# Row statistics moved from VectorE to ScalarE, in whole rows, and one combination from GpSimd to VectorE

## The chip, the cores and the metric

The kernel runs on one core of a Trainium2 chip. A core has TensorE (matrix products into the accumulation memory, PSUM), VectorE, ScalarE and GpSimd for elementwise work, and SyncE, which issues almost all transfers between the device memory and the on-chip memory, SBUF. Each engine works through its own queue in the order in which the program wrote it; engines meet through semaphores. In the profile they are called PE (and PEld for its weight loads), DVE, ACT, POOL and SP. The metric is the device time of one execution in microseconds; the time before is 2860.64 us, the median of 3 runs (2856.56 to 2867.07).

## What is computed

x is 128 batches of 128 tokens with 768 features; adj is 128 matrices of 128 x 128 edge weights, most of them zero. Per batch the kernel computes a normalised and clipped x, one attention layer with 12 heads of 64 features masked by the edges, and adds the result to x:

```
h      = maximum(layernorm(x), 0)                  # mean and variance over the 768 features of a token
q, k, v = h @ Wq + bq, h @ Wk + bk, h @ Wv + bv    # 768 x 768 each, split into 12 heads
scores = q @ k.T / sqrt(64) + beta * adj           # per head, 128 x 128
scores = where(adj > 0, scores, -9e15)
out    = x + softmax(scores) @ v
```

Everything is float32. The layer norm needs two numbers for each token, its mean and its variance; these are the row statistics of the title. The row sums of the title are the denominators of the softmax: each v has a 65th column of ones, so the product of exponentials and v carries the sum of the exponentials in that column.

## The kernel before

**Groups, slices and products.** The 128 batches are taken in 32 groups of four. For each group the projections are computed in three slices of columns: qk0 (q and k of the first six heads), v, and qk1 (q and k of the last six). Each slice is a fast product of 2 x 3 blocks of activations with 3 x 3 blocks of weights, with 15 block products (`PRODUCTS`) in place of 18; each block product in turn uses seven half-size products, called zones, in place of eight. So a slice is 15 positions, taken in the order `ZORDER` (qk0 and v) or `QORDER` (qk1), and a group is 45 positions. Order of slices in the steady loop: qk0, v, qk1, then qk0 of the next group.

The operands of a product are a sum of activation blocks (prepared on VectorE and GpSimd by `sum_acts` and `inner`) and a sum of weight blocks. The weight sums are made once; 11 of the 45 stay in SBUF and 34 are read again for each group from device memory through a ring of five buffers (`load_T`, 448 KB each). The load of the next one is issued by SyncE when a product has freed its buffer, that is, some seven positions ahead of its use.

**Chains and homes.** Each product belongs to one of four chains a, b, c, d (third column of `PRODUCTS`) and is accumulated on top of the products of its chain in one pair of PSUM banks; there are four pairs. The next product of a chain overwrites what the readers of the one before still need, so TensorE waits until they have read. The readers are in `product_z`. Each output block (r, j) has a home in SBUF, seven zones wide. The first product that touches a home is copied there, mainly by ScalarE (lines 560, 563 and 565; two zones of v by VectorE, line 559); each further one is added by VectorE (line 569). When a home is complete, `decode` combines its seven zones into four, on GpSimd (lines 585 to 588 for q and k, 596 to 600 for v), one or four positions later. In ZORDER position 6 copies into a home of v, position 9 is on chain a as position 6 is, and position 13 is on chain d as position 10 is. In QORDER position 0 opens two homes at once, with two runs of lines 563 and 565, and position 3 is the next product of its chain, d.

**Attention.** `scores` makes the products of q and k for two heads of the four batches (line 622), `mask` adds the edge bias on VectorE (line 630), ScalarE takes the exponential (line 632). `attend` multiplies with v between the zones of a product (line 675); ScalarE copies the result with its row sums out of PSUM (line 684, which frees the bank pair); two positions later `weigh` clips and inverts the sums on VectorE (lines 645 and 646), ScalarE scales by them (line 658), VectorE adds x (line 698). The scores and the attention of the second half of a group's heads are interleaved with qk0 of the next group: scores at positions 3, 5 and 6.

**Layer norm.** Activations are read in a transposed block form, 32 tokens at a time, by `load_x`; `norm` applies scale, shift and clipping on ScalarE (line 446), and `to_hT` transposes on VectorE (line 457). The scale and shift come from statistics of the plain rows: for group G + 2, during slice v of group G (for group 2, during qk0 of group 1), `load_half` reads each batch in two halves of 384 features into three buffers in turn, `half_stats` takes VectorE's statistics of a half (line 415) and joins two halves (line 417), and `row_moments` turns the eight results into scale and shift (lines 423 to 430), which are brought into the block form through device memory.

**Order.** The order of the work is written out by hand. `run` goes through the positions; `then(at, f, ...)` puts f behind the matmuls of position `at`, and `then((at, "post"), ...)` behind its evacuation and behind the exponentials and scalings that trail it. What is put there takes its place in the queue of whichever engine it runs on: a load in SyncE's, ahead of the weight load of the next position.

Of the kernel before, what the change touches and what calls it, by code (L numbers as in the profile page):

```python
# [125 lines left out]
def direct(ctx, tc, x, adj, wq, bq, wk, bk, wv, bv, beta, out, bad):  # L126
# [39 lines left out]
    def flat(lo, hi):  # L166
        return sbig[:, lo:hi]
# [36 lines left out]
    ones = const.tile([P, P], F32, name="ones")  # L204
    nc.gpsimd.memset(ones, 1.0)
    beta_s = const.tile([P, 1], F32, name="beta_s")

# [190 lines left out]

    def load_half(G, n):

        g, h = n // 2, n % 2
        if n % 3 == 2:
            t = work.tile([P, VH], F32, tag="adj", name=f"half_{G}_{g}_{h}", bufs=1)
        else:
            t = half_homes[n % 3]
        rows[G, g, h] = t
        nc.sync.dma_start(t, x[G * GRP + g, :, h * VH:(h + 1) * VH])

    def half_stats(G, n):

        g, h = n // 2, n % 2
        if n == 0:
            rows[G] = stat.tile([P, GRP, 2, nc.vector.BN_STATS_DIM], F32, tag="strow", name=f"strow_{G}", bufs=1)
            rows[G, "mv"] = stat.tile([P, GRP, nc.vector.BN_AGGR_DIM], F32, tag="mvrow", name=f"mvrow_{G}", bufs=1)
        nc.vector.bn_stats(rows[G][:, g, h, :], rows.pop((G, g, h)))  # L415
        if h:
            nc.vector.bn_aggr(rows[G, "mv"][:, g, :], rows[G][:, g])

    def row_moments(G, first=5, then=8):

        mv = rows[G, "mv"]
# [107 lines left out]
    def product_z(G, sl, n):  # L529
# [21 lines left out]
        for (r, j), sign in uses:  # L551
# [85 lines left out]

    def weigh(G, oc, pa, o):

        n = pa.shape[1]  # L640
# [3 lines left out]
        t = sums[G][:, oc]  # L644
        nc.vector.tensor_scalar(t[:, 0, 0:n], pa[:, :, :, HD], TINY, None, op0=ALU.max)
        nc.vector.reciprocal(t[:, 1, 0:n], t[:, 0, 0:n])  # L646
# [18 lines left out]
    def attend_steps(G, oc, behind):  # L665
# [16 lines left out]

        def leave_pair():
            nc.scalar.copy(o.rearrange("p r b e -> p r (b e)"), pair[:, :, 0:4 * VE])  # L684
            give(pair)
            later(weighed_later, 2)

        def weighed_later():
            divide = weigh(G, oc, o, o)
# [350 lines left out]
    for G in range(1, NG):  # L1040
# [6 lines left out]
        if G == 1:  # L1047
            sums_at(1, ((0, "S6"), (1, "S7"), (2, "S0"), (5, "S5"), (7, "S14"), (9, "S11")))
            then((0, "post"), load_x, 2, 0)
            for n, at in enumerate((1, 1, 1, 6, 8, 9, 11, 11)):  # L1050
                then((at, "post"), load_half, 2, n)
            for n, at in enumerate((6, 8, 9, 10, 11, 12, 13, 14)):
                then(at, half_stats, 2, n)
            then(14, row_moments, 2, 3, 5)
# [14 lines left out]
        if more:  # L1069
            then((11, "post"), add_raw, G + 1)  # L1070
            if G == 1:
                for g in range(2):
                    then((6 + g, "post"), norm, 2, g)
                turn_act(2, ((9, "A01"), (10, "A00"), (11, "A02")), 1)
                then((11, "post"), load_x, 2, 1)
                then((14, "post"), norm, 2, 2)
# [17 lines left out]
        if G == 1:  # L1094
            then((0, "post"), norm, 2, 3)
# [160 lines left out]
```

## Time and profile before

| | |
|---|---|
| median of 3 runs | 2860.64 us (2856.56 to 2867.07) |
| profiled execution | 2872.12 us, span 2870.3 us, mean granted TensorE clock 0.984 |
| TensorE busy | 2727.4 us, 95% of the span |
| VectorE busy | 2319.8 us, 81% |
| GpSimd busy | 2202.8 us, 77% |
| ScalarE busy | 1496.6 us, 52% |
| transfers | 721.72 MB, mean 251 GB/s |
| chain that ended last, by engine | GpSimd 42%, TensorE 27%, VectorE 12%, DMA 11% |

The prediction quotes lines of the profile. A group line gives the line of the kernel, the engine, the operation, output and input tiles with their shapes and the count; then busy time in us and the mean of one in ns; then the idle time of the engine just ahead of these instructions, and what ended it. A line of the waits names who waited for whom, with the total in us, the times and the longest. A line of the timeline gives start and length in us, and in square brackets an idle time ahead of it with its releaser. A line of transfers gives the tile, the count, the size and the median time from issue to landing. A busy share is a mean over the span; a wait counts where it stops the engine that is the bound. The lines of before: L415 and L417 are the statistics of halves, L645 the clipping of row sums, L585 to L588 the combination of a q/k home.

### The profile page before, as it was taken

To read this page: it belongs to the slowest core of one execution; us is meant where nothing else is said; L and a number is where in the kernel's file an instruction comes from. 1 tells how busy PE (TensorE), PEld (TensorE's weight loads), DVE (VectorE), ACT (ScalarE), POOL (GpSimd) and SP (SyncE) were. 2 spreads that over 40 slices of the span, in tenths; PEclk is the share of its full clock that TensorE was granted. 3 is DMA by queue.
4 is the path that set the end of the run, shared out by engine and by line. 5 is a ranking of instruction groups with operands and counts; after the bars stand their busy time and mean duration, and the time that the engine had idled before them with its cause. 6 is when DMAs were issued, how large, how long until landed. Compare 5 with 4: busy or idle time off the path is not lost.

```text
span 2870.3 us, 121387 instructions
## 1 busy us (share of the span) xinstructions
PE 2727.4 (95%) x52029; PEld 2598.4 (91%) x52029; DVE 2319.8 (81%) x3148; ACT 1496.6 (52%) x3823; POOL 2202.8 (77%) x3169
## 2 busy tenths in 40 slices
PE   9989999999999999999999999999999999999998
PEld 7789998999999999989899999899898999998997
DVE  6878888887878788888788888788887887878885
ACT  1455655455555555554555554555545555555654
POOL 4667878777878778787778787778787787877885
PEclk9999999999999999999999999999999999999999
DMA  8779878888888898788888888888887888978875
GB/s 214 252 241 275 263 238 270 247 262 260 232 260 262 250 268 263 239 270 251 250 274 248 253 265 253 259 258 239 263 263 244 267 236 251 273 240 266 247 229 164
DMA packets 547620, 721.72 MB, mean 251 GB/s; under 512 B 107900, under 2 KB 406664, under 8 KB 547080
## 3 DMA queue, kind: packets, MB, share of 16 engines
q1 hardware_dynamic: 545920, 713.13, 82.2%
q8 instruction: 412, 6.75, 0.9%
q10 hardware_dynamic: 1160, 0.79, 0.1%
q14 instruction: 128, 1.05, 0.1%
HBM read 647.73 MB, written 66.05 MB: 249 GB/s over the span
## 4 chain that ended last, share of the span: by engine, by line
POOL 42%; PE 27%; DVE 12%; DMA 11%; issue 4%; ACT 2%; SPq 0%; POOLq 0%; DVEq 0%; ACTq 0%
PE pair L545 22%; DMA sbig<-in_x_dram 9%; POOL home L586 6%; POOL home L588 5%; POOL home L585 4%; POOL v L600 4%; DVE home L569 4%; POOL home L587 4%; POOL home L598 4%; PE pair L675 3%; DVE strow L415 3%; POOL v L599 3%; PE pair L622 2%; POOL A L467 2%; POOL home L597 2%
## 5 line engine op out<-in xcount | busy, mean ns | idle before, releaser
L569 DVE TENSOR_TENSOR home<-home,pair 128x896 f32<-128x896 f32 x810 | 857.9, 1072 | 200.2 <-PE pair L545 177.6
L545 PE MATMUL pair<-sbig,T_qk 128*64 128x128 f32 x13888 | 887.3, 273 | 3.3 <-DMA T_qk<-kept_qk 1.7
L545 PEld LDWEIGHTS pair<-sbig,T_qk 128*64 128x64 f32 x13888 | 754.7, 137 | 17.2 <-issue 10.0
L658 ACT ACTIVATE e<-e,sm 128x64 f32<-128x64 f32 x1512 | 382.2, 339 | 242.1 <-DVE sm L646 242.1
L545 PE MATMUL pair<-A,T_qk 128*64 128x128 f32 x6076 | 425.0, 278 | 0.0
L585 POOL TENSOR_TENSOR home<-home 128x256 f32<-128x256 f32 x325 | 259.1, 797 | 215.8 <-DVE home L569 213.0
L545 PE MATMUL pair<-T_v,sbig 128*64 128x128 f32 x6944 | 413.8, 274 | 3.0 <-DVE sbig L569 3.0
L675 PE MATMUL pair<-v,e 128*64 128x65 f32 x6048 | 404.1, 223 | 2.8 <-DVE e L630 2.8
L545 PEld LDWEIGHTS pair<-T_v,sbig 128*64 128x64 f32 x6944 | 385.0, 137 | 8.6 <-issue 5.3
L563 ACT ACTIVATE home<-pair 128x640 f32<-128x640 f32 x325 | 228.3, 703 | 303.1 <-PE pair L545 299.0
L675 PEld LDWEIGHTS pair<-v,e 128*64 128x64 f32 x6048 | 363.3, 139 | 6.8 <-DVE e L630 3.3
L545 PEld LDWEIGHTS pair<-A,T_qk 128*64 128x64 f32 x6076 | 338.9, 140 | 5.5 <-issue 5.3
L588 POOL TENSOR_TENSOR home<-home 128x256 f32<-128x256 f32 x325 | 291.4, 897 | 25.5
L586 POOL TENSOR_TENSOR home<-home 128x256 f32<-128x256 f32 x325 | 289.7, 891 | 25.5
L632 ACT ACTIVATE e<-e 128x1024 f32<-128x1024 f32 x189 | 200.3, 1060 | 185.0 <-DVE e L630 172.7
L630 DVE SCALAR_TENSOR_TENSOR e<-pair,biasT 128x1024 f32<-128x1024 f32 x189 | 229.8, 1216 | 61.4 <-PE pair L622 61.0
L684 ACT COPY e<-pair 128x520 f32<-128x520 f32 x189 | 111.5, 590 | 316.7 <-PE pair L675 316.7
L446 ACT ACTIVATE x<-x,block 128x192 f32<-128x192 f32 x480 | 231.8, 543 | 10.2 <-DMA x<-in_x_dram 10.2
L622 PE MATMUL pair<-home 64*64 64x128 f32 x5312 | 201.1, 279 | 36.4 <-POOL home L587 23.4
L587 POOL TENSOR_TENSOR home<-home 128x128 f32<-128x128 f32 x325 | 207.8, 639 | 25.5
L467 POOL TENSOR_TENSOR A<-A 128x256 f32<-128x256 f32 x186 | 153.2, 824 | 89.2 <-DVE A L457 89.1
L545 PE MATMUL pair<-T_v,A 128*64 128x128 f32 x2604 | 167.0, 281 | 56.4 <-DVE home L569 47.7
(178 smaller groups left out, 4616.2 us busy)
## 6 DMA issues: line engine op xcount, KB each, us to landing
T_qk<-kept_qk SPq DMA_DIRECT2D x713, 448.0 KB, 4.8
T_v<-kept_v SPq DMA_DIRECT2D x341, 448.0 KB, 5.7
xo<-in_x_dram SPq DMA_DIRECT2D x189, 256.0 KB, 4.3
out_dram<-xo SPq DMA_DIRECT2D x189, 256.0 KB, 5.7
x<-in_x_dram SPq DMA_DIRECT2D x248, 192.0 KB, 5.8
sbig<-in_x_dram SPq DMA_DIRECT2D x186, 192.0 KB, 5.2
half<-in_x_dram SPq DMA_DIRECT2D x60, 192.0 KB, 3.9
kept_qk<-prep_qk SPq DMA_DIRECT2D x23, 448.0 KB, 3.1
```

What stands on the lines that cost most here:

```text
L446: nc.scalar.activation(t, t, AF.Relu, bias=shift[G, n], scale=rstd[G, n])
L545: nc.tensor.matmul(p[q:q + HD, at, :], lhs[:, q:q + HD], rhs, start=(first and at % 4 == 0), stop=True, skip_group_check=True)
L563: nc.scalar.activation(t[:, 0:5], p[:, 0:5], AF.Copy, scale=float(sign))
L569: nc.vector.tensor_tensor(t, t, p[:, 0:7], op)
L585: e.tensor_tensor(t[:, 1:4:2], t[:, 1:4:2], twice(5), ALU.add)
L586: e.tensor_tensor(t[:, 2:5:2], t[:, 2:5:2], twice(1), ALU.add)
L587: e.tensor_tensor(t[:, 4], t[:, 4], t[:, 6], ALU.add)
L588: e.tensor_tensor(t[:, 0:7:6], t[:, 0:7:6], twice(2), ALU.add)
L622: nc.tensor.matmul(ps[k:k + HD, i, g * N:(g + 1) * N], keys[r, k:k + HD], queries[r], start=True, stop=True)
L630: nc.vector.scalar_tensor_tensor(e, ps, SCORE_CAP * ISCALE, bias, op0=ALU.min, op1=ALU.add)
L658: nc.scalar.activation(o[:, r, b, 0:HD], pa[:, r, b, 0:HD], AF.Copy, scale=t[:, 1, r, b:b + 1])
L675: nc.tensor.matmul(pa[q:q + HD, 2 * g + i, :], k[:, q:q + HD], vt[G, "v", r, h // 4][:, 4 * g + h % 4, :], start=True, stop=True, skip_gro ...
```

## The change

Three edits, with the positions of the work around them moved to fit:

- **Row statistics.** A whole row of 768 features is read into one buffer, where the first two half-row buffers stood (the third, in the tile `adj`, is no longer used). ScalarE makes two passes over it, both written back in place: a copy that accumulates the sum, then a square of the row less its mean that accumulates the squared deviations; between them a multiplication of one column makes the negative mean. `row_moments` takes these. A row can be loaded when the second pass over the row before has ended. In the steady loop the first row of a group is loaded at position 12 of qk0, the others at 2, 6 and 11 of v; the statistics stand behind positions 1, 5, 10 and 14 of v. The normalisations of the second pair of batches move from positions 5, 6, 8, 9 of v to 3, 4, 7, 8.
- **Row sums.** ScalarE reads the column of sums from PSUM, adds 1e-30 and writes it, ahead of the copy of line 684; VectorE's clipping (line 645) goes, except in the last group's half-size steps.
- **One combination.** The home completed by product 13 of qk1 (position 12), block (1, 2), is combined by VectorE in place of GpSimd.

```diff
-    half_homes = [flat(spare + i * D // 2, spare + (i + 1) * D // 2) for i in range(2)]
+    row_home = flat(spare, spare + D)
...
+    def load_row(G, g):
+        nc.sync.dma_start(row_home, x[G * GRP + g])
+
+    def row_stats(G, g):
+
+        if g == 0:
+            rows[G] = stat.tile([P, 3, GRP], F32, tag="strow", name=f"strow_{G}", bufs=1)
+        s = rows[G]
+        nc.scalar.activation(row_home, row_home, AF.Copy, accum_out=s[:, 0, g:g + 1])
+        nc.scalar.mul(s[:, 1, g:g + 1], s[:, 0, g:g + 1], -1.0 / D)
+        nc.scalar.activation(row_home, row_home, AF.Square, bias=s[:, 1, g:g + 1], accum_out=s[:, 2, g:g + 1])
...
-        nc.vector.tensor_scalar(ve, mv[:, :, 1], EPS, None, op0=ALU.add)
-        mean = stat.tile([P, GRP], F32, tag="meanrow", name=f"meanrow_{G}", bufs=1)
-        nc.vector.tensor_scalar(mean, mv[:, :, 0], -1.0, None, op0=ALU.mult)
+        nc.vector.tensor_scalar(ve, rows[G][:, 2], 1.0 / D, EPS, op0=ALU.mult, op1=ALU.add)
+        mean = rows[G][:, 1]
...
-                later(lambda r=r, j=j: decode(G, sl, r, j), 1 if order_of(G, sl) is LORDER else LAG.get((sl, n), 1))
+                later(lambda r=r, j=j: decode(G, sl, r, j, nc.vector if (sl, n) == ("qk1", 13) else nc.gpsimd), 1 if order_of(G, sl) is LORDER else LAG.get((sl, n), 1))
...
         def leave_pair():
+            nc.scalar.activation(row_sums(G, oc)[:, 0], pair[:, :, 0:4 * VE].rearrange("p r (b e) -> p r b e", e=VE)[:, :, :, HD],
+                                 AF.Identity, bias=tiny)
             nc.scalar.copy(o.rearrange("p r b e -> p r (b e)"), pair[:, :, 0:4 * VE])
...
+                if G + 2 < NG:
+                    then((12, "post"), load_row, G + 2, 0)
...
-                for n, at in enumerate((5, 6, 8, 9)):
+                for n, at in enumerate((3, 4, 7, 8)):
                     then((at, "post"), norm, G + 1, 2 + n // 2, n % 2 * 2, n % 2 * 2 + 2)
...
-                for n, at in enumerate((0, 0, 0, 4, 4, 5, 7, 9)):
-                    then((at, "post"), load_half, G + 2, n)
-                for n, at in enumerate((4, 4, 5, 7, 9, 9, 11, 12)):
-                    then(at, half_stats, G + 2, n)
+                for g, at in enumerate((0, 4, 8, 11) if G == 1 else (None, 2, 6, 11)):
+                    if at is not None:
+                        then((at, "post"), load_row, G + 2, g)
+                for g, at in enumerate((3, 6, 10, 14) if G == 1 else (1, 5, 10, 14)):
+                    then((at, "post"), row_stats, G + 2, g)
```

Group 1, which prepares group 2 in its own qk0 slice, has other positions for the same work: rows loaded at 1, 5, 9 and 12 of qk0 with the statistics at 4, 8, 11 and 14, `row_moments` moved from position 14 of qk0 to 0 of v, the first two normalisations of group 2 at 7 and 8 of v (before 6 and 7), its transpositions and the load of its second pair one position later each, and the third normalisation moved from v to qk1.

More of the change, by code (lines that the diff above doesn't have):

```diff
@@ L205, in direct @@
     nc.gpsimd.memset(ones, 1.0)
+    tiny = const.tile([P, 1], F32, name="tiny")
+    nc.gpsimd.memset(tiny, TINY)
     beta_s = const.tile([P, 1], F32, name="beta_s")
@@ L636, in direct, with row_sums @@
     sums, weighed = {}, {}
-    def weigh(G, oc, pa, o):
-        n = pa.shape[1]
+    def row_sums(G, oc):
         if G not in sums:
@@ L643, in weigh @@
             weighed[G] = 0
-        t = sums[G][:, oc]
-        nc.vector.tensor_scalar(t[:, 0, 0:n], pa[:, :, :, HD], TINY, None, op0=ALU.max)
+        return sums[G][:, oc]
+    def weigh(G, oc, pa, o, summed=False):
+        n = pa.shape[1]
+        t = row_sums(G, oc)
+        if not summed:
+            nc.vector.tensor_scalar(t[:, 0, 0:n], pa[:, :, :, HD], TINY, None, op0=ALU.max)
         nc.vector.reciprocal(t[:, 1, 0:n], t[:, 0, 0:n])
@@ L1049, in direct @@
             then((0, "post"), load_x, 2, 0)
[L1050 to L1054, printed above, removed]
+            for g, at in enumerate((1, 5, 9, 12)):
+                then((at, "post"), load_row, 2, g)
+            for g, at in enumerate((4, 8, 11, 14)):
+                then((at, "post"), row_stats, 2, g)
         else:
@@ L1071, in direct @@
             if G == 1:
+                then(0, row_moments, 2, 3, 5)
                 for g in range(2):
[L1073 to L1076, printed above, removed]
+                    then((7 + g, "post"), norm, 2, g)
+                turn_act(2, ((10, "A01"), (11, "A00"), (12, "A02")), 1)
+                then((12, "post"), load_x, 2, 1)
             else:
-                for n, at in enumerate((5, 6, 8, 9)):
+                for n, at in enumerate((3, 4, 7, 8)):
                     then((at, "post"), norm, G + 1, 2 + n // 2, n % 2 * 2, n % 2 * 2 + 2)
@@ L1094, in direct @@
         if G == 1:
-            then((0, "post"), norm, 2, 3)
+            for g in range(2, GRP):
+                then((g - 2, "post"), norm, 2, g)
             turn_act(2, ((3, "A10"), (4, "A11"), (5, "A12")), 1)
```

19 lines of the change are left out of this document (1 added, 18 removed).

## The prediction

> **What bounds the kernel now.** I read the page's busy shares first, then TensorE's waits, then one group stage by stage and in order of time. All prices below belong to one steady group of four batches: the one whose v slice begins at 1131 us.
>
> ```profile
> PE 2727.4 (95%) x52029; PEld 2598.4 (91%) x52029; DVE 2319.8 (81%) x3148; ACT 1496.6 (52%) x3823; POOL 2202.8 (77%) x3169
> ```
> ```profile
> PE pair L545 <- DVE home L569: 48.0, 26, 2.0
> PE pair L622 <- POOL home L587: 23.4, 21, 1.2
> PE pair L545 <- DVE e L630: 12.0, 20, 1.5
> PE pair L545 <- DVE sbig L569: 11.8, 6, 3.0
> PE pair L622 <- POOL home L588: 10.3, 27, 0.5
> ```
> TensorE is busy 95% of the span, so no edit to another engine can win more than its waits and what they do to its clock. The five rows of TensorE's waits (us, times, longest) sum to 105.5 us. They come once a group each, at two places: a product of the v slice waits for VectorE, and the scores in the next qk0 slice wait for GpSimd.
>
> In order of time (start us, us, [idle before <- releaser]), first TensorE, then VectorE:
>
> ```profile
> 1148.58 1.70 PE L545 MATMUL pair<-T_v,sbig 128*64 128x128 f32 x28
> ...
> 1156.96 1.75 PE L545 MATMUL pair<-T_v,A 128*64 128x128 f32 x28 [1.97 <-DVE home L569]
> ...
> 1164.65 1.70 PE L545 MATMUL pair<-A,res_qk 128*64 128x128 f32 x28
> ...
> 1201.30 0.45 PE L622 MATMUL pair<-home 64*64 64x128 f32 x8 [1.23 <-POOL home L587]
> 1202.10 0.45 PE L622 MATMUL pair<-home 64*64 64x128 f32 x8 [0.35 <-POOL home L588]
> 1202.48 2.62 PE L545 MATMUL pair<-A,T_qk 128*64 128x128 f32 x28
> ```
> ```profile
> 1147.23 0.56 DVE L415 BATCH_NORM_STATS2 strow<-sbig 128x6 f32<-128x384 f32 x1 [2.18 <-DMA sbig<-in_x_dram]
> ```
> The rows are v position 9, v position 13 (1.97 us late), qk1 position 3, and the scores of qk0 (1.23 + 0.35 late); a product takes 1.53 us from start to start. VectorE is late at position 13 because at 1145 it stood 2.18 us for a half row to land.
>
> Two stretches of it (length, then busy us of TensorE, its weight loads, VectorE, ScalarE and GpSimd; granted clock, DMA share, GB/s), and the whole span:
>
> ```profile
> 1133.00:1160.40 27.40, 25.43 (x495) 24.18 (x489) 21.12 (x33) 11.07 (x19) 19.63 (x35) 1.00 0.97 307
> ...
> 1190.00:1219.80 29.80, 28.00 (x551) 26.25 (x548) 22.38 (x29) 18.93 (x50) 19.57 (x27) 0.94 0.72 214
> ```
> ```profile
> core 0: 2870.3 us, clock 0.984
> ```
> In the v slice (first row) ScalarE works 11.07 of 27.40 us and the DMA engines are 0.97 busy. In the qk0 stretch the granted clock is 0.94, a loss of 1.8 us, and the first product after the GpSimd wait takes 2.62 us where its like take 1.70: a half-rate stretch follows the wait. Over the span 1.6% of 2870 is 46 us; by estimate 28 of them, 1.0 per steady group, are these stretches, and the rest lies in the start and the tail.
>
> **The change part by part.**
>
> The groups of instructions, costliest first (busy us, then mean ns of one | idle us before them and what ended it):
>
> ```profile
> L569 DVE TENSOR_TENSOR home<-home,pair 128x896 f32<-128x896 f32 x810 | 857.9, 1072 | 200.2 <-PE pair L545 177.6 <-POOL home L597 5.0 <-ACT e L632 3.7
> ...
> L588 POOL TENSOR_TENSOR home<-home 128x256 f32<-128x256 f32 x325 | 291.4, 897 | 25.5
> L586 POOL TENSOR_TENSOR home<-home 128x256 f32<-128x256 f32 x325 | 289.7, 891 | 25.5
> L585 POOL TENSOR_TENSOR home<-home 128x256 f32<-128x256 f32 x325 | 259.1, 797 | 215.8 <-DVE home L569 213.0 <-DVE sm L645 2.9
> L446 ACT ACTIVATE x<-x,block 128x192 f32<-128x192 f32 x480 | 231.8, 543 | 10.2 <-DMA x<-in_x_dram 10.2
> L630 DVE SCALAR_TENSOR_TENSOR e<-pair,biasT 128x1024 f32<-128x1024 f32 x189 | 229.8, 1216 | 61.4 <-PE pair L622 61.0
> ...
> L587 POOL TENSOR_TENSOR home<-home 128x128 f32<-128x128 f32 x325 | 207.8, 639 | 25.5
> L565 ACT ACTIVATE home<-pair,bqk 128x128 f32<-128x128 f32 x650 | 202.8, 370 | 0.0
> ...
> L632 ACT ACTIVATE e<-e 128x1024 f32<-128x1024 f32 x189 | 200.3, 1060 | 185.0 <-DVE e L630 172.7 <-POOL prep_qk L284 6.5 <-POOL A L467 5.4
> ...
> L698 DVE TENSOR_TENSOR xo<-xo,e 128x512 f32<-128x512 f32 x189 | 185.5, 982 | 3.4 <-ACT e L658 3.4
> ...
> L457 DVE STREAM_TRANSPOSE A<-x 128x512 f32<-128x512 f32 x186 | 129.9, 699 | 54.5 <-ACT x L446 54.5
> ...
> L415 DVE BATCH_NORM_STATS2 strow<-sbig 128x6 f32<-128x384 f32 x180 | 97.5, 553 | 87.0 <-DMA sbig<-in_x_dram 86.6
> ...
> L645 DVE TENSOR_SCALAR sm<-e 128x8 f32<-128x8 f32 x189 | 73.0, 386 | 4.5 <-ACT e L684 1.3
> ...
> L486 ACT ACTIVATE adj<-adj,beta_s 128x512 f32<-128x512 f32 x32 | 24.1, 753 | 7.0 <-DMA kept_v<-prep_v 3.7 <-DVE biasT L485 3.2
> ...
> L486 ACT ACTIVATION_READ_ACCUMULATOR adj<-adj,beta_s 128x1 f32 x32 | 7.4, 230 | 0.0
> ...
> L279 DVE TENSOR_TENSOR prep_qk<-prep_qk 128x128 f32<-128x128 f32 x17 | 6.5, 381 | 0.0
> ...
> L341 ACT ACTIVATE tables<-nhalf 128x1 f32<-128x1 f32 x1 | 0.2, 203 | 0.0
> ```
> *VectorE.* Gone per group: 8 x 0.553 = 4.4 us of half-row statistics with their aggregates, 6 x 0.386 = 2.3 us of row sums, and the waits for landings (L415's 87.0 us idle, 2.9 a group). Added: one home's combination, three ops of 128x256 and one of 128x128 with both inputs in SBUF. No row has 128x256 on VectorE; between 0.381 (128 wide) and 0.982 (512) it is 0.58, so 2.1 us in all. Its cover is qk0's idle 7.4 us; without it the additions of qk1 positions 13 and 14 leave their banks 2.1 us late, against two positions (3.06 us) before that bank's chain is needed.
>
> *GpSimd.* Gone: 0.797 + 0.891 + 0.639 + 0.897 = 3.22 us per group, ahead of the combination that the scores at 1201 wait for.
>
> *ScalarE, row statistics.* 768 wide lies midway between 0.753 (512) and 1.060 (1024): 0.91. Two such passes, two accumulator reads of 0.23 and a 128x1 multiply of 0.20 make 2.48 us a row, 9.9 a group; v holds 16.3 idle.
>
> *ScalarE, row sums.* A 128x8 op between 0.203 and 0.370, say 0.29, six times: 1.7 us. It stands ahead of the copy that frees the bank pair. Bounds 0 to 1.7 us; I take 0, as no row of TensorE's large waits is for that copy.
>
> *The new waits.* There is one row buffer, so a load stands in SyncE's queue until ScalarE has ended the row before, with the loads of prepared weights queued behind it; and ScalarE, in its own order, stands for the landing, with the evacuations of later products behind it. How long a 384 KB row takes to land no row shows; the nearest, from the page's DMA issues (KB each, median us to landing):
>
> ```profile
> T_qk<-kept_qk SPq DMA_DIRECT2D x713, 448.0 KB, 4.8
> T_v<-kept_v SPq DMA_DIRECT2D x341, 448.0 KB, 5.7
> ...
> sbig<-in_x_dram SPq DMA_DIRECT2D x186, 192.0 KB, 5.2
> half<-in_x_dram SPq DMA_DIRECT2D x60, 192.0 KB, 3.9
> ```
> Bounds 3.9 and 5.7. I take 5.2 for rows 1 and 2, in the crowded part of v, and 4.4 (midway between 3.9 and 4.8) for row 3, which is issued after SyncE has stood and the queues have drained.
>
> ```profile
> 1136.70 1.05 ACT L632 ACTIVATE e<-e 128x1024 f32<-128x1024 f32 x1
> ...
> 1161.87 0.70 ACT L563 ACTIVATE home<-pair 128x640 f32<-128x640 f32 x1 [7.68 <-PE pair L545]
> ...
> 1163.56 0.65 ACT L565 ACTIVATE home<-pair,bqk 128x128 f32<-128x128 f32 x2
> ```
> The chain through v, in this group's times. Row 0 is loaded in qk0 and has landed; its statistics follow the exponential: 1137.75 to 1140.2. Row 1 is issued then, lands 1145.4, ends 1147.9. Position 6's copy (0.70) ends 1148.6, when position 9 starts at 1148.58: no loss. Then VectorE's addition (1.07) and mask (1.22) end at 1150.9, the exponential 1152.0, a pair of normalisations (1.09) 1153.0, position 9's copy 1153.7. Row 2 (issued 1147.9, landed 1153.1) runs to 1156.2. VectorE meanwhile transposes (0.70) after those normalisations and makes position 10's two additions by 1155.9; position 13, which could start at 1154.99, starts then instead of at 1156.96. Row 3 is issued 1156.2, lands 1160.6, ends 1163.1. Only then come the four copies that free chain d at qk1 position 0 (2.34 us, first to last in the fence): 1165.4. Position 3 of qk1 needs them and would be ready at 1163.6; it waits 1.8 us and starts 0.75 us later than today's 1164.65. That is what is late next.
>
> The weights behind row 2 on SyncE go out at 1148.3 instead of 1146 and land by 1154.0, a microsecond or two ahead of position 13: no cost, but 1 us a group if landings lengthen by two.
>
> *At nothing.* Row loads move the same bytes in four pieces for eight, and the first now goes out behind qk0's x loads, one more issue on SyncE ahead of one weight load (some 0.4 us, within the microseconds that weights land early). One small op of the moments goes; one memset comes, once. The normalisations are as many, one or two positions earlier, and stand in the chain above.
>
> *Scores.* GpSimd starts its unbroken stretch 1 us earlier (1155.9 for 1156.9) and is 3.22 us shorter, TensorE comes 0.75 us later: the wait of 1.58 us goes.
>
> *Clock.* The half-rate stretches after that wait go (1.0 a group); the 1.8 us wait at qk1 brings some back, as today's 1.97 us waits seldom do: 0.3 by estimate. Net 0.7. The Trainium skill ("TensorE: Matmul & The Clock Gate", the table of Part 1) lets the clock drop after an idle window of about 3.4 us and its closing table asks for no gaps over about 3 us. Here the half rate follows 1.58 us of waits among 64-wide score matmuls, so the trace does not agree; by the rule alone shorter gaps would not change the clock.
>
> **Sum.** 0.75 - 1.58 - 0.7 = -1.5 us a group; 28 groups make -42. Group 1 and the tail I leave at nothing. The profiled execution took 2872.1 us (span 2870.3), 11.5 above the median of 2860.64; so 2819 on the median's scale.
>
> **The rivals.**
> - *Rows land as fast as the half buffer's 3.9 us.* The v and qk1 waits all but go; position 3 starts 1.0 us before today: (-1.0 - 1.58 - 1.0) x 28 = -101, 2760. For it: larger pieces and a stopped SyncE. Against: DMA 0.97 busy in v.
> - *The half-rate stretches stay as they are*, since other causes put them there: 0.7 x 28 = 20 less gain, 2839.
> - *The move off GpSimd does not reach TensorE.* VectorE's new ops slow GpSimd's neighbours as much as they relieve it, or the last combination waits for its own data: 1.58 x 28 = 44 less, 2863, no change. The Trainium skill ("GPSIMD Engine Reference", Specifications) has GpSimd's SBUF interface shared with VectorE's two-input instructions, which speaks for this; no run before shows this op there.
> - *Slower: ScalarE's chain of landings.* One mechanism, at qk1 position 3: each microsecond more in rows 1 and 3 together (9.6 above) moves position 3 by one. From 11.1 on, the gain is eaten. With both at the 5.7 us of the v weights (11.4), the chain is 2.55 late, the wait there is about 3.6 us and a half-rate stretch (1.7) follows each: 2.55 - 1.58 - 1.0 + 1.7 = 1.7 a group, 47 us, 2907. For it: VectorE waited for such loads already, and in two buffers more. Against: ScalarE's idle 16 us, and the extra spacing of the loads.
>
> **How the numbers follow.** The likeliest 0.40, alone 2795 to 2845; fast landings 0.10; clock unchanged 0.07; no relief at the scores 0.15; slower 0.28. Half a percent, 14 us, is about what a measurement of this kernel can tell from no change: faster 0.57, same 0.15, slower 0.28. The range 2755 to 2900 leaves out the best of the fast landings and the worse half of the slow case.
>
> **What would show it.** Right: no TensorE wait for VectorE over 1 us in v, a wait of 1 to 3 us at qk1 position 3 for ScalarE's copies, none for GpSimd at the scores, ScalarE idle for row landings, SyncE standing at the row load, a clock of 0.985 to 0.99. Wrong: row statistics far from 2.5 us, weights landing late for TensorE, or the scores still waiting.

## The result, and the profile after

The changed kernel takes 2823.11 us (median of 4 runs, 2815.93 to 2829.78) against 2858.6 us of the kernel before in the same series (4 runs, 2848.44 to 2867.07): a ratio of 0.9877, with a 95% interval of 0.9835 to 0.9918. The prediction was 2819. A second series on one chip gave 2835.81 us (6 runs, 2817.39 to 2854.61) and 0.9906 [0.9876, 0.9937]. The change is worth about 1%.

The page's first line of the changed kernel, its chain of work that ended last by engine, and the span with its granted clock:

```profile
PE 2698.8 (96%) x52029; PEld 2584.4 (92%) x52029; DVE 2144.0 (76%) x2693; ACT 1760.0 (62%) x4612; POOL 2078.3 (74%) x3046
```
```profile
PE 67%; DVE 9%; ACT 9%; DMA 5%; issue 4%; POOL 2%; SPq 2%; ACTq 0%; DVEq 0%; POOLq 0%
```
```profile
core 0: 2823.3 us, clock 0.989
```

Between the two profiled executions the span fell by 47.0 us. Of these, 28.6 us are TensorE's own busy time (2727.4 to 2698.8, the same 52029 matmuls, at a granted clock of 0.989 for 0.984) and 18.4 us its idle time (142.9 to 124.5, span less busy). The clock accounts for some 15 of the 28.6 us (1.6% of 2870 less 1.1% of 2823); what the rest is stays open. GpSimd's part in the last chain went from 42% to 2%. TensorE's waits of the changed kernel (who waited for whom: us, times, longest):

```profile
PE pair L537 <- ACT home L557: 68.3, 44, 3.5
PE pair L537 <- ACT sbig L557: 15.4, 9, 3.3
PE pair L719 <- POOL home L579: 4.2, 2, 2.3
...
PE pair L614 <- issue: 2.9, 8, 0.8
PE pair L537 <- DVE home L561: 2.9, 1, 2.9
```

(Lines are renumbered: L537 is the product, before L545; L614 the scores, before L622; L557 the last of the copies that open a home, before L565; L561 VectorE's additions, before L569; L577 to L580 the combination, before L585 to L588; L642 the reciprocal, before L646; L654 ScalarE's scaling, before L658; L409 to L411 the new row statistics.) Both waits of before are gone: v for VectorE (48.0 us) has one case left, the scores for GpSimd none but two in the last group (L719), which the kernel before had too. A new wait, for ScalarE's copies, stands in their place.

One steady group in order of time (start, length in us, [idle before <- releaser]); its v slice begins at 1030.70. SyncE's row loads, then ScalarE, then TensorE:

```profile
1028.61 0.45 SPq L402 DMA_DIRECT2D sbig<-in_x_dram  x1
1039.48 0.33 SPq L402 DMA_DIRECT2D sbig<-in_x_dram  x1
1046.06 0.33 SPq L402 DMA_DIRECT2D sbig<-in_x_dram  x1
1053.17 2.02 SPq L468 DMA_DIRECT2D adj<-in_adj_dram  x4
1055.29 0.86 SPq L402 DMA_DIRECT2D sbig<-in_x_dram  x1
```
```profile
1059.78 0.85 ACT L409 ACTIVATE sbig<-sbig 128x768 f32<-128x768 f32 x1 [6.22 <-DMA sbig<-in_x_dram]
...
1061.92 0.68 ACT L555 ACTIVATE home<-pair 128x640 f32<-128x640 f32 x1
...
1063.58 0.64 ACT L557 ACTIVATE home<-pair,bqk 128x128 f32<-128x128 f32 x2
```
```profile
1055.65 1.70 PE L537 MATMUL pair<-res_v,A 128*64 128x128 f32 x28
...
1064.28 3.26 PE L537 MATMUL pair<-A,res_qk 128*64 128x128 f32 x28 [2.34 <-ACT home L557]
```

The fourth row is issued at 1055.29, behind the four loads of the adjacency, and lands 4.5 us later. ScalarE stands 6.22 us for it, then makes the statistics, then the four copies; TensorE's qk1 position 3 waits 2.34 us for these, and its product runs at half rate (3.26 us for 1.70). In the median of 26 steady groups this wait is 2.7 us. The first product in the fence is v position 14: it starts 24.95 us into v, in the group of before 27.42 us (1158.54 less 1131.12).

### The profile page after: what moved, and what is told of

It is laid out like the page before. It is cut to its first block, busy times and chain, and to the rows that moved or that the text cites. A ratio compares the mean times of both kernels' runs of the same rounds, so it can differ in the third digit from the quotient of the medians.

```text
span 2823.3 us, 121538 instructions
## 1 busy us (share of the span) xinstructions
PE 2698.8 (96%) x52029; PEld 2584.4 (92%) x52029; DVE 2144.0 (76%) x2693; ACT 1760.0 (62%) x4612; POOL 2078.3 (74%) x3046
## 3 DMA queue, kind: packets, MB, share of 16 engines
q14 instruction: 129, 1.06, 0.1%
## 4 chain that ended last, share of the span: by engine, by line
PE 67%; DVE 9%; ACT 9%; DMA 5%; issue 4%; POOL 2%; SPq 2%; ACTq 0%; DVEq 0%; POOLq 0%
PE pair L537 56%; PE pair L614 6%; PE pair L671 5%; DMA sbig<-in_x_dram 4%; DVE home L561 3%; ACT e L654 2%; ACT home L555 2%; ACT home L557 1%; SPq L468 1%; DVE sbig L454 1%; ACT sbig L409 1%; DVE xo L696 1%; ACT sbig L411 1%; DVE sbig L561 1%; POOL home L577 0%
## 5 line engine op out<-in xcount | busy, mean ns | idle before, releaser
L561 DVE TENSOR_TENSOR home<-home,pair 128x896 f32<-128x896 f32 x810 | 861.1, 1076 | 394.2 <-PE pair L537 198.9
L537 PE MATMUL pair<-sbig,T_qk 128*64 128x128 f32 x13888 | 892.4, 274 | 0.0
L537 PEld LDWEIGHTS pair<-sbig,T_qk 128*64 128x64 f32 x13888 | 759.5, 138 | 11.8 <-issue 6.5
L577 POOL TENSOR_TENSOR home<-home 128x256 f32<-128x256 f32 x299 | 247.8, 829 | 356.6 <-DVE home L561 344.6
L654 ACT ACTIVATE e<-e,sm 128x64 f32<-128x64 f32 x1512 | 382.1, 340 | 184.3 <-DVE sm L642 183.5
L537 PE MATMUL pair<-A,T_qk 128*64 128x128 f32 x6076 | 414.5, 273 | 0.0
L537 PE MATMUL pair<-T_v,sbig 128*64 128x128 f32 x6944 | 412.4, 273 | 0.7 <-ACT home L552 0.3
L537 PEld LDWEIGHTS pair<-T_v,sbig 128*64 128x64 f32 x6944 | 383.6, 137 | 6.7 <-issue 4.5
L537 PEld LDWEIGHTS pair<-A,T_qk 128*64 128x64 f32 x6076 | 330.0, 137 | 5.5 <-issue 5.5
L580 POOL TENSOR_TENSOR home<-home 128x256 f32<-128x256 f32 x299 | 268.5, 898 | 23.5
L537 PE MATMUL pair<-A,res_qk 128*64 128x128 f32 x2604 | 196.0, 287 | 73.2 <-ACT home L557 58.6
L622 DVE SCALAR_TENSOR_TENSOR e<-pair,biasT 128x1024 f32<-128x1024 f32 x189 | 230.4, 1219 | 38.5 <-PE pair L614 38.0
L578 POOL TENSOR_TENSOR home<-home 128x256 f32<-128x256 f32 x299 | 240.0, 803 | 23.4
L680 ACT ACTIVATE sm<-pair,tiny 128x8 f32<-128x8 f32 x189 | 49.9, 264 | 332.2 <-PE pair L671 332.2
L579 POOL TENSOR_TENSOR home<-home 128x128 f32<-128x128 f32 x299 | 214.7, 718 | 23.4
L537 PE MATMUL pair<-sbig,res_qk 128*64 128x128 f32 x3472 | 214.5, 275 | 14.7 <-ACT home L557 9.7
L537 PEld LDWEIGHTS pair<-A,res_qk 128*64 128x64 f32 x2604 | 149.9, 145 | 80.5 <-ACT home L557 64.8
```

What stands on the lines that cost most here:

```text
L537: nc.tensor.matmul(p[q:q + HD, at, :], lhs[:, q:q + HD], rhs, start=(first and at % 4 == 0), stop=True, skip_group_check=True)
L561: nc.vector.tensor_tensor(t, t, p[:, 0:7], op)
L577: e.tensor_tensor(t[:, 1:4:2], t[:, 1:4:2], twice(5), ALU.add)
L578: e.tensor_tensor(t[:, 2:5:2], t[:, 2:5:2], twice(1), ALU.add)
L579: e.tensor_tensor(t[:, 4], t[:, 4], t[:, 6], ALU.add)
L580: e.tensor_tensor(t[:, 0:7:6], t[:, 0:7:6], twice(2), ALU.add)
```

## The experiments

All times are medians; ratios are to the kernel before in the same series, with 95% intervals. "Busy" and "idle" are TensorE's in the profiled execution, idle being the span less busy.

| kernel | us | ratio | busy | idle |
|---|---|---|---|---|
| before | 2858.6 to 2868.5 | 1 | 2727.4 | 142.9 |
| the change | 2823.1; 2835.8 | 0.9877; 0.9906 | 2698.8 | 124.5 |
| statistics alone | 2827.9 | 0.9879 [0.9859, 0.9899] | 2698.9 | 120.8 |
| combination alone | 2913.5 | 1.0163 [1.0141, 1.0185] | 2731.2 | 183.9 |
| row sums alone | 2850.7 | 0.9960 [0.9946, 0.9973] | 2708.9 | 136.1 |
| the change, combination undone | 2815.6; 2816.7 | 0.9837 [0.9818, 0.9856]; 0.9833 [0.9813, 0.9854] | 2695.3 | 113.6 |
| the change, row sums undone | 2886.1 | 1.0067 [1.0045, 1.0090] | 2712.4 | 166.4 |
| the change without loads of rows 1 to 3 | 2763.0 | 0.9644 [0.9627, 0.9662] | 2675.3 | 90.0 |
| the change, fourth row's load first | 2787.4 | 0.9740 [0.9724, 0.9757] | 2680.3 | 102.3 |
| the change, fourth row's statistics later | 2778.0 | 0.9697 [0.9676, 0.9718] | 2678.4 | 96.2 |
| the same, combination undone | 2775.8 | 0.9696 [0.9679, 0.9712] | 2688.9 | 85.6 |
| the same, combination on VectorE later | 2786.1 | 0.9710 [0.9693, 0.9727] | 2684.6 | 99.4 |

**Which part carries the gain?** The row statistics alone, and the combination alone, each put into the kernel before. The first is the change less its edits in `leave_pair`, `weigh` and `decode`'s call; the second is one line:

```diff
-                later(lambda r=r, j=j: decode(G, sl, r, j), 1 if order_of(G, sl) is LORDER else LAG.get((sl, n), 1))
+                later(lambda r=r, j=j: decode(G, sl, r, j, nc.vector if (sl, n) == ("qk1", 13) else nc.gpsimd), 1 if order_of(G, sl) is LORDER else LAG.get((sl, n), 1))
```

> The kernel before with the first edit alone: row statistics by ScalarE, with the moved positions; row sums and the combination as before. If the wait at qk1 position 3 comes from the chain of row landings, it is here as in the changed kernel (2 to 3 us a group) and the wait in v for VectorE is gone. If the combination's move is what relieved the scores, their wait for GpSimd of 1 to 1.6 us a group is still here and the time is about 2823 + 45 to 65 = 2870 to 2885. If GpSimd's earlier start in v relieved them, the wait is not here and the time is 2820 to 2835.

> The kernel before with the third edit alone: the home completed by product 13 of qk1 is combined by VectorE. By the prediction's own step (GpSimd's unbroken stretch ends 3.22 us earlier, so the scores no longer wait) the wait of 1.58 us and most of the half-rate stretches behind it go: (1.58 + 0.7) x 28 = 64 us, about 2795; the wait of 1.97 us in v stays. By the rival, that the last combination waits for its own data from VectorE, or VectorE is later by its 1.6 us of new work, the scores still wait and the time is that of before, 2850 to 2870.

The statistics alone give the whole gain (0.9879), and the time lies in the 2820 to 2835 us expected for the case that GpSimd's earlier start in v relieves the scores. GpSimd there does all the work that it did before, and still the scores do not wait for it. In time order, GpSimd's first operation after it stood for VectorE in v, in the kernel before (v from 1131.12) and with the statistics alone (v from 1026.78); then, with the statistics alone, GpSimd's last operation ahead of the scores, and the scores:

```profile
1155.02 0.72 POOL L467 TENSOR_TENSOR A<-A 128x256 f32<-128x256 f32 x1 [3.03 <-DVE A L457]
```
```profile
1048.56 0.73 POOL L459 TENSOR_TENSOR A<-A 128x256 f32<-128x256 f32 x1 [0.93 <-DVE A L449]
...
1094.75 0.73 POOL L580 TENSOR_TENSOR home<-home 128x256 f32<-128x256 f32 x1
```
```profile
1095.75 1.10 PE L614 MATMUL pair<-home 64*64 64x128 f32 x32
```

GpSimd starts 21.78 us into v for 23.90 before, 2.1 us earlier, and keeps that: in the medians of 26 steady groups it ends its last combination 69.2 us into v for 71.4 before, while TensorE, its wait there left out, comes to the last of these scores at 70.3 for 70.2.

The combination alone takes the scores' wait away too, and costs 1.6%: 2913.5 us, above both times expected. Its trace, VectorE, ScalarE and TensorE in qk0 of one group:

```profile
1117.88 0.95 DVE L585 TENSOR_TENSOR home<-home 128x256 f32<-128x256 f32 x1
...
1120.20 0.42 DVE L588 TENSOR_TENSOR home<-home 128x256 f32<-128x256 f32 x1
...
1122.14 0.70 DVE L645 TENSOR_SCALAR sm<-e 128x8 f32<-128x8 f32 x1
1122.88 0.20 DVE L646 RECIPROCAL sm<-sm 128x8 f32<-128x8 f32 x1
```
```profile
1123.18 2.02 ACT L658 ACTIVATE e<-e,sm 128x64 f32<-128x64 f32 x8 [5.11 <-DVE sm L646]
1125.10 0.68 ACT L563 ACTIVATE home<-pair 128x640 f32<-128x640 f32 x1
1125.68 0.61 ACT L565 ACTIVATE home<-pair,bqk 128x128 f32<-128x128 f32 x2
```
```profile
1126.34 3.25 PE L545 MATMUL pair<-sbig,res_qk 128*64 128x128 f32 x28 [2.81 <-ACT home L565]
```

The 2.7 us of combination stand in VectorE's queue ahead of the clipping and the reciprocal of the row sums. ScalarE waits 5.11 us for these, and behind its scaling stand the copies for which TensorE then waits 2.81 us, with a half-rate product after it. VectorE had idle time in qk0, but not ahead of the reciprocal. TensorE comes to the last scores 3.4 us later than before in this kernel (73.6 us into v), so it does not show by itself that the shorter GpSimd work relieves them.

**Row sums alone**, the edits in `leave_pair` and `weigh` put into the kernel before:

> The kernel before with the row sums alone moved from VectorE to ScalarE (0.26 us each on ScalarE ahead of the copy that frees a pair, 0.29 us each off VectorE behind it). The prediction took the two at nothing: 2855 to 2868 us, ratio 0.998 to 1.002. The theory that the row sums matter, since the reciprocal and the scaling behind them come 0.29 us earlier and ScalarE's copies wait for these: a gain of 0.1 to 0.4 us a group, 2850 to 2860 us, ratio 0.996 to 0.999. The opposite (ScalarE's queue is 4 x 0.26 us longer a group, and TensorE waits for the pairs that it frees): a loss of up to 1 us a group, up to 2890 us, ratio up to 1.01.

2850.7 us: a gain of 0.4%, more than the prediction's nothing, and within the 2850 to 2860 of the theory that the row sums matter. The clipping on VectorE, ahead of the reciprocal, takes 0.70 us at the place shown above; ScalarE's own read of the sums takes 0.264 us (mean of 189 in the changed kernel). How the 13 us divide between this chain and the clock stays open.

**Each of the two undone in the changed kernel**, beside the changed kernel itself:

```diff
-                later(lambda r=r, j=j: decode(G, sl, r, j, nc.vector if (sl, n) == ("qk1", 13) else nc.gpsimd), 1 if order_of(G, sl) is LORDER else LAG.get((sl, n), 1))
+                later(lambda r=r, j=j: decode(G, sl, r, j), 1 if order_of(G, sl) is LORDER else LAG.get((sl, n), 1))
```
```diff
-            nc.scalar.activation(row_sums(G, oc)[:, 0], pair[:, :, 0:4 * VE].rearrange("p r (b e) -> p r b e", e=VE)[:, :, :, HD],
-                                 AF.Identity, bias=tiny)
...
-            divide = weigh(G, oc, o, o, True)
+            divide = weigh(G, oc, o, o)
```

> The changed kernel with the one moved combination (qk1, position 13) given back to GpSimd; the other two parts stay. The prediction's step (the scores' wait of 1.58 us a group goes because GpSimd's stretch is 3.22 us shorter): the wait comes back in part or whole, so 28 groups x 0.8 to 1.58 us = 22 to 44 us more than the changed kernel, 2845 to 2867 us, ratio to before 0.995 to 1.003. The theory after the run of the combination alone (GpSimd is relieved by starting earlier, and has 1.48 and 4.60 us idle in qk1 of the changed kernel, where the combination fits; on VectorE it only delays the row sums and the copies behind them): no scores wait above 0.5 us a group, 2805 to 2830 us, ratio 0.981 to 0.990, and the ScalarE waits of qk0 (15.4 us in 9) smaller or gone. It is the first theory's if the wait of the scores for GpSimd stands among TensorE's waits with more than 20 us.

> The changed kernel with the combination on GpSimd, beside the changed kernel. If the combination on VectorE costs the changed kernel something (the small waits for ScalarE's copies in qk0, some 15 to 20 us in the trace of the changed kernel less those that this one still has): 5 to 15 us faster than the changed kernel of the same call. If it is neutral there, both within 4 us.

> The changed kernel with the row sums given back to VectorE: the statistics and the combination, without the row sums. If the parts add, the row sums' 0.4% are missing: 0.9877 / 0.996 = 0.992, 2830 to 2845 us. If the relief of VectorE by the row sums is what makes the combination bearable there (alone it cost 1.6%), more comes back: 2850 to 2875 us, ratio 0.996 to 1.004. If the row sums are worth nothing beside the other two, 2815 to 2828 us.

> The changed kernel as it is, beside the others on one chip, so that the parts can be set against it: 2816 to 2830 us, ratio 0.984 to 0.990.

The changed kernel itself came out above the 2816 to 2830 us expected. Without the combination the kernel is faster, by 19 us in the series that ran both (2816.7 and 2835.8; the intervals do not touch). The first pair, from two series, is closer (0.9837 and 0.9877, and the intervals overlap). TensorE hardly waits for GpSimd at the scores, 1.8 us in the last row:

```profile
PE pair L537 <- ACT home L557: 59.7, 24, 4.0
PE pair L537 <- ACT sbig L557: 11.8, 5, 3.1
...
PE pair L614 <- POOL home L580: 1.8, 4, 0.5
```

Without the row sums the gain turns into a loss, 2886.1 us, more than any of the three theories expected: the wait for ScalarE's copies grows, and comes a second time in each group, in qk0:

```profile
PE pair L537 <- ACT home L557: 105.5, 49, 4.3
PE pair L537 <- ACT sbig L557: 19.2, 10, 3.2
```
```profile
1108.12 0.70 DVE L641 TENSOR_SCALAR sm<-e 128x8 f32<-128x8 f32 x1
1108.85 0.20 DVE L642 RECIPROCAL sm<-sm 128x8 f32<-128x8 f32 x1
```
```profile
1112.32 1.75 PE L537 MATMUL pair<-sbig,res_qk 128*64 128x128 f32 x28 [1.27 <-ACT home L557]
```

So the two parts hang together: the combination costs 1.9% beside the statistics (1.0067 / 0.9879, from two series), and 0.4 to 0.7% once the clipping no longer stands between it and the reciprocal (0.9877 / 0.9837 and 0.9906 / 0.9833).

**What does the wait at qk1 position 3 hang on?** Three kernels: one that leaves out the loads of rows 1 to 3 of the steady groups; one that issues the fourth row's load ahead of the adjacency; one that makes the fourth row's statistics behind qk1 position 0, after the copies.

```diff
-                    if at is not None:
+                    if at is not None and G == 1:
```
```diff
-            then((11, "post"), add_raw, G + 1)
...
                     if at is not None:
                         then((at, "post"), load_row, G + 2, g)
+            then((11, "post"), add_raw, G + 1)
```
```diff
-                for g, at in enumerate((3, 6, 10, 14) if G == 1 else (1, 5, 10, 14)):
+                for g, at in enumerate((3, 6, 10, 14) if G == 1 else (1, 5, 10)):
...
+            if G + 2 < NG:
+                then((0, "post"), row_stats, G + 2, 3)
```

> The changed kernel without the loads of rows 1 to 3 in the steady loop: ScalarE makes all its passes, over what stands in the buffer, and waits for no landing (the statistics of those rows are therefore not those of x). By the theory the wait at qk1 position 3 falls from 2.3 to 3.3 us to under 0.5 and the time to about 2750 to 2765; 5% of the transfers are gone too. By the rival, that the passes themselves (2.2 us a row) are too much for ScalarE, the wait stays above 1.5 us and the time above 2800.

> The changed kernel with one order changed: in the steady groups the load of the fourth row is issued ahead of the four loads of the adjacency at v position 11, not behind them. Nothing else moves. If the wait of 2.3 us at qk1 position 3 hangs on the landing of that row, the row lands some 1.8 us earlier (the time by which SP issues it later now is about 2 us), ScalarE's two passes end as much earlier and 28 x 1.2 to 1.8 us go, with the half rate behind them: 2770 to 2795 us, ratio 0.967 to 0.977, and TensorE's wait for the home copies falls from 68 us under 40 us. If the landing is bound by the bytes that are under way with it, not by the place in the queue, the row lands as late as now: 2815 to 2830 us. If the adjacency, 1.2 us later, holds up the additions that read it, a wait of VectorE or GpSimd takes its place: above 2830 us.

> The changed kernel with one thing moved: in the steady loop the statistics of the fourth row stand behind qk1 position 0 instead of v position 14, so ScalarE makes the four copies of qk1 position 0 first. By the theory (the copies stand behind a row that has not landed) TensorE's wait of 2.3 to 3.3 us at qk1 position 3 goes, with half-rate stretches: about 2.7 x 28 = 75 us, near 2750. By the rival, that ScalarE simply has too much work there, the wait moves to a later position and the time stays within 20 us of 2823.

With no landing to wait for and all passes still made, the wait in qk1 is gone and the time is 2763.0 us, 60 less: the landings, not ScalarE's work, hold TensorE up, though some of the 60 us may belong to the transfers that are left out. The two other kernels leave nothing out. With the load first, the row no longer stands behind the adjacency's 2.21 us of issue, and TensorE's wait in qk1 (first of the TensorE rows) is a third in this group, and 1.1 us for 2.6 in the mean of 26 groups:

```profile
1042.83 0.33 SPq L402 DMA_DIRECT2D sbig<-in_x_dram  x1
1043.21 2.21 SPq L468 DMA_DIRECT2D adj<-in_adj_dram  x4
```
```profile
1051.51 1.75 PE L537 MATMUL pair<-A,res_qk 128*64 128x128 f32 x28 [0.78 <-ACT home L557]
...
1078.67 1.75 PE L537 MATMUL pair<-sbig,res_qk 128*64 128x128 f32 x28 [1.22 <-ACT home L557]
```

The time is as expected (2787.4 of 2770 to 2795). The total of the waits for these copies, 47.7 us in 48 cases, stayed above the 40 expected, because of a second one in qk0 (the second row). With the statistics moved behind the copies the wait in qk1 is gone, the clock is 0.997, and the kernel is faster than with the load first: 2778.0 us. It stayed 28 us above the 2750 expected. What is left is the wait in qk0 (first row; the second is VectorE's additions):

```profile
PE pair L537 <- ACT home L557: 31.0, 25, 1.5
PE pair L537 <- DVE home L561: 16.9, 25, 2.1
```

**Is the combination in VectorE's queue what is left?** In that last kernel the combination is given back to GpSimd (the diff above), or stays on VectorE two slots later, behind the reciprocal:

```diff
-LAG = {("v", 8): 4, ("v", 12): 4, ("qk1", 11): 4}
+LAG = {("v", 8): 4, ("v", 12): 4, ("qk1", 11): 4, ("qk1", 13): 3}
```

> The kernel with the fourth row's statistics behind qk1 position 0, with the combination of qk1 position 13 given back to GpSimd. In that kernel VectorE makes the combination from 1066.0 to 1068.3 us of the profiled run, behind it the reciprocal at 1069.87, for which ScalarE's scaling waits 3.37 us, and behind that the copies for which TensorE waits 1.22 us in each group (31.0 us in 25). GpSimd is idle 2.14 us ahead of the next combination. Theory that the combination on VectorE costs this wait: it goes, 25 x 1.2 = 31 us, less up to 0.3 us a group where GpSimd ends 1.1 us later than its slack of 0.9 us: 2745 to 2765 us, ratio 0.959 to 0.966. Theory that GpSimd needs the relief: the scores wait 1 us or more a group again, 2780 to 2805 us, ratio 0.971 to 0.980.

> The kernel with the fourth row's statistics behind qk1 position 0; the combination stays on VectorE, and stands there two slots later, behind the reciprocal of the row sums and the first additions of qk0 instead of ahead of them. If the 2.2 us of combination ahead of the reciprocal make the wait of 1.24 us for ScalarE's copies in qk0 (reciprocal, scaling, copies, TensorE), the reciprocal comes about 2.2 us earlier, the wait goes, and GpSimd stays relieved: 25 x 1.24 = 31 us less than the 2778 us of that kernel, 2740 to 2755 us, ratio 0.957 to 0.963, and neither ScalarE's copies of the homes nor GpSimd's combinations stand among TensorE's waits with over 15 us. If it is the scaling itself (2.0 us on ScalarE) that is in the way of the copies, at most 0.3 us a group go: 2768 to 2780 us. If the scores wait for the combination that now ends some 4 us later, or the additions behind it free the banks too late, a wait of VectorE takes its place: above 2780 us.

Both take the wait for the copies in qk0 away, so the combination is its cause; neither gives the 31 us back. On GpSimd (first fence) the scores wait again, 14.0 and 11.0 us; on VectorE later (second fence) the additions and the edge bias (L622) come late:

```profile
PE pair L537 <- DVE home L561: 16.0, 24, 2.0
PE pair L614 <- POOL home L579: 14.0, 24, 0.7
PE pair L614 <- POOL home L580: 11.0, 28, 0.8
```
```profile
PE pair L537 <- DVE home L561: 29.0, 50, 2.1
PE pair L614 <- DVE e L622: 27.4, 31, 2.5
```

Both expectations of a gain were wrong (2775.8 us lies in neither range of the first): at each of the three places tried the 2 to 3 us of the combination leave a wait behind.

## Why the prediction was right, and where its steps were wrong

**Right in kind, too small: v.** "Position 13 ... starts then instead of at 1156.96" gave 1.06 us a group. The wait went altogether; v position 14 starts 2.5 us earlier into v, because VectorE no longer stands for landings. The prediction read its five rows of waits as two places; the 12.0 us for L630 are a third, 19 us into v, and fall to 2.0.

**Right: what is late next.** The chain of landings, statistics and copies ahead of qk1 position 3 was predicted with 1.8 us of wait; it measured 2.34 in the group shown and 2.7 in the median, the more so because TensorE arrives there earlier. So position 3 starts 33.58 us into v in the group shown, for 33.53 before, where 0.75 us later was predicted: v's larger gain pays for the longer wait. The terms of the chain: the fourth row issued 25.1 us into v predicted, 24.6 measured; landing 4.4 predicted, 4.5 measured. The 5.2 taken for the second and third rows was too much: their medians are 4.6 and 4.1 us (the first row, loaded in qk0, takes 7.3). A row's statistics were priced at 2.48 us; the groups give 0.838 + 0.190 + 0.203 + 0.936 + 0.186 = 2.35:

```profile
L411 ACT ACTIVATE sbig<-sbig,strow 128x768 f32<-128x768 f32 x120 | 112.3, 936 | 3.9
L409 ACT ACTIVATE sbig<-sbig 128x768 f32<-128x768 f32 x120 | 100.6, 838 | 194.7 <-DMA sbig<-in_x_dram 194.6
...
L410 ACT ACTIVATE strow<-strow 128x1 f32<-128x1 f32 x120 | 24.4, 203 | 3.8
L409 ACT ACTIVATION_READ_ACCUMULATOR sbig<-sbig 128x1 f32 x120 | 22.8, 190 | 0.0
L411 ACT ACTIVATION_READ_ACCUMULATOR sbig<-sbig,strow 128x1 f32 x120 | 22.4, 186 | 0.0
```

The Trainium skill ("ScalarE: Activation LUTs", What ACT_TABLE_LOAD costs) gives 186 ns and 0.833 ns an element, 93 ns more for a bias read from a column: 826 and 920 ns by estimate for 768. The trace agrees, within 2%.

**Right in size, in part by luck: the sum.** -42 us was predicted, -35 and -33 measured in the two series. By the profiled spans the waits gave 18.4 us (predicted 0.83 x 28 = 23) and the clock some 15 (predicted 0.7 x 28 = 20); the other 14 us of busy time stand in no term. The luck is in the three steps below: the relief at the scores came without the part that it was put down to, and two parts that were taken at nothing nearly cancel. (The sum of the fast rival makes -100, not -101.)

**Wrong: the scores.** "GpSimd starts its unbroken stretch 1 us earlier ... and is 3.22 us shorter": the shortening was not what took the wait away. The statistics alone do it, and so does the changed kernel with the combination undone. By its own terms the prediction did not need it: GpSimd 1 us earlier and TensorE 0.75 us later make 1.75 us, for a wait of 1.58. The earlier start was the right half, and was 2.1 us. The shortening brings GpSimd's end in the changed kernel only from 69.1 to 68.7 us into v. What the prediction overlooked is that TensorE gains in v as well. It loses this gain again at qk1 position 3, and so comes to the scores no earlier than before. Where that hold-up is gone (the fourth row's statistics later) the combination does decide: on GpSimd, which ends at 68.7 us into v while TensorE comes at 68.0, the scores wait 25.0 us, 0.9 us a group, against 33.7 in the two rows of before; on VectorE they do not wait for GpSimd, but TensorE waits 31.0 us for the copies in qk0. The rival "the move off GpSimd does not reach TensorE" was right that the move brings nothing, and wrong on the price, since the scores' wait went without it.

**Wrong: the cover of VectorE's combination.** "Its cover is qk0's idle 7.4 us" counted idle time over the stretch, and looked for who waits only in the additions. Behind the combination stand the reciprocal, ScalarE's scaling and the copies. Its duration was over-priced (2.1 us; 0.527 + 0.441 + 0.293 + 0.425 = 1.69 in the groups of the changed kernel, though 0.900 + 0.558 + 0.639 + 0.425 = 2.52 where it stands alone), its effect under-priced: nothing predicted; 1.6% alone and 0.4 to 0.7% in the whole.

**Wrong: the row sums at nothing.** They are worth 0.4% alone and 1.6% beside the combination (1.0067 to 0.9906), because what leaves VectorE there stands ahead of the same reciprocal. This error and the one before it nearly cancel in the whole change: statistics alone 0.9879, everything 0.9877 and 0.9906.

The slower rival, ScalarE's chain of landings, has the mechanism that the runs without loads and with the load first show: it costs about 36 to 60 us of what the change could give. It stayed below its point of decision, 11.1 us for rows 1 and 3 together (the second and the fourth): they landed in 4.6 and 4.5 us.

## What to carry to other kernels

Idle time of an engine over a stretch is no cover for added work: follow the added operation to the next one behind it in its queue, and from that to who waits. Undo each part of a change as well as trying it alone; here a part that is worth 0.4% alone holds 1.6% in company, and a part that costs is hidden by the gain of another. Where a load must land ahead of work that frees a buffer, look at its place in the issuing queue and at the place of its consumer: moving one step gave about 36 and 45 us here.

## What the runs showed of the hardware that was not expected

The half-rate stretch after a wait depends on the wait's length, and on where the wait falls. In the fourteen profiles of this case, between 120 and 2760 us, the products of 28 matmuls that started after a wait, counted by the wait; the last column counts those that took over 1.95 us, where the undisturbed ones take 1.70 to 1.75:

| wait, us | products | over 1.95 us |
|---|---|---|
| 0.4 to 1.5 | 325 | 0 |
| 1.5 to 2.0 | 159 | 23 |
| 2.0 to 2.5 | 43 | 22 |
| 2.5 to 3.0 | 86 | 48 |
| over 3.0 | 61 | 44 |

So a wait that is cut from 2.5 to 1 us gives back more than its own length; in the table of the experiments TensorE's busy time mostly falls with its idle time (not in "the same, combination undone").

Which of the longer waits are followed by it can be read from the granted clock. In these traces it is full or half, never between; between 120 and 2760 us every half-rate stretch lasts 3.41 us or twice that, and in each trace all of them begin on one grid with steps of 3.41 us. What counts is TensorE's idle time in one step. Five steps of the changed kernel (from and to, length, TensorE's busy us; granted clock, DMA share, GB/s):

```profile
715.84:719.25 3.41, 2.02 (x38) 1.00 0.99 352
719.25:722.66 3.41, 1.83 (x34) 1.00 0.77 291
722.66:726.08 3.42, 3.42 (x83) 1.00 0.07 12
...
1060.58:1063.99 3.41, 1.35 (x26) 1.00 0.91 288
1063.99:1067.40 3.41, 3.12 (x30) 0.50 0.58 226
```

A wait of 2.97 us that ended at 720.83 lies across two steps, 1.39 and 1.58 us idle, and the full rate goes on. The wait of 2.34 us shown above has 2.06 us in one step, and the next step is at half rate. Over the fourteen traces a half-rate step followed all 118 steps with over 2.02 us idle, 23 of the 54 with 1.90 to 2.02, and 26 of the 3608 with less; of these 26, 13 were at half rate already, and 11 hold the score waits of the kernel before (1.58 us). By estimate from the 3.41 and the 2.02 us, a wait of 2.25 us at a random place is followed by the half rate in 47% of the cases and one of 2.75 us in 62%; the table has 51% and 56%.

The Trainium skill ("TensorE: Matmul & The Clock Gate", What's actually happening) lets the clock drop after an idle window of about 3.4 us, and lets this window run freely. The traces agree with a window that runs freely, of 3.41 us. They do not agree that all of it has to be idle: 2.02 us of it were enough each time.
